# Turning a normalized tile on TensorE: GpSimd scales it before plain transposes, or TensorE multiplies by diagonals of 1/sigma

## Chip, cores and metric

The kernel runs on one core of a Trainium2 chip. The metric is the time of one execution on the device, in microseconds (us); a kernel's time is the median of several runs. TensorE is called PE here (PEld is its loading of weights), VectorE DVE, ScalarE ACT, GpSimd POOL and SyncE SP, as in the profile. L321 is line 321 of the kernel.

## What is computed

Two layers run one after the other on an input of 8 images of 128 x 128 positions with 128 channels, all in float32. The change lies in layer 0, an attention with a linear cost followed by a normalization over the channels:

```python
qkv = jnp.einsum('bhwc,cf->bhwf', x, w_qkv)
q, k, v = jnp.split(qkv, 3, axis=-1)          # 4 heads of 32
q = jax.nn.softmax(q, axis=-2) * inv_scale    # over the 32 of a head
k = jax.nn.softmax(k, axis=-1)                # over the positions of an image
context = jnp.einsum('bhdn,bhen->bhde', k, v)
attn = jnp.einsum('bhde,bhdn->bhen', context, q)
out = jnp.einsum('bhwf,fc->bhwc', attn, w_out) + b_out
mu = jnp.mean(out, axis=-1, keepdims=True)
var = jnp.mean(jnp.square(out - mu), axis=-1, keepdims=True)
out = (out - mu) * jax.lax.rsqrt(var + LN_EPS) * gamma + beta
return out + x
```

Layer 1 is a scan over the image in four orders (a selective state-space layer). It takes three quarters of the time, and the change doesn't touch it.

## The kernel before, in words

`layer0` keeps two images in SBUF, channels on the partitions (`xs`), and works on groups of 4 columns of 128 positions, that is on 128 x 512 tiles; an image has 32 groups. The function `image(b)` writes out by hand the order in which the stages of three images are interleaved: it attends to image `b`, it gathers the context (the product of keys and values) of image `b + 1`, and it computes the gate of image `b - 1`, which layer 1 needs. In step `t` it calls the stages for groups `t`, `t - 1`, `t - 2` and so on, so each group passes through several steps. `in_order` ties every instruction to the one before it on its engine, so each engine's queue holds exactly this order.

In one step PE gets these products, in this order: `pq` (L268, queries of group `t`), `pg` (L288, the exponentials of the queries times the output weights), `pk` (L180, keys of the next image), `pv` (L225, its values), `po` (L294, through the context), `pc` (L240, adds to the next image's context) and `pt` (L321, the turn). Each product of float32 appears as two records in the trace. All outputs of PE but `pc` and `pmx` rotate through 6 banks of PSUM.

The keys' softmax needs a maximum. Every four groups (`BK = 4`) the stages `fold` and `spread` take it: DVE reduces a tile (L196, L197), PE turns it (L206, `pmt`, a transpose), DVE reduces the result, joins it to the last maximum (L208, L210, L212), and writes a diagonal (L214, `dg`); PE spreads it over the partitions (L219, `pmx`). This is called a fold below.

A group's way through the attention is: `query` (PE L268; on DVE the maximum L270 and the subtraction L272), `exponent` (ACT L275), `normalize` (DVE L280, L281; POOL L282, which multiplies the tile by the reciprocals), `through_wo` (PE L288, ACT copy `gt` L290), `through_context` (PE L294; DVE adds the bias, L296, and writes the tile `o`; ACT squares it into `sq`, L298), `variance` (DVE L302), `scale` (POOL L308, L310, L313), `turn` (PE L321) and `finish` (ACT L325 applies gamma and beta, POOL L327 adds the input, and SP stores two groups at a time to DRAM, L330). The mean is taken out of the weights beforehand, so `o` has none.

After the normalization the tile must be turned, from positions on the partitions back to channels. Before the change, `scale` writes into a tile `d` four diagonal matrices that hold 1/sigma, one for each column of the group, and `turn` multiplies: the tile `o` of a column, as the stationary operand, times its diagonal gives the tile turned and scaled at once.

```python
i3 = ident.rearrange("p (o c) -> p o c", o=1)
nc.gpsimd.tensor_tensor(
    d, i3.to_broadcast([P, GW, P]), rstd.to_broadcast([P, GW, P]), ALU.mult
)
```

Image 0's context comes alone, before any attention. Images 0 to 6 have attention and context side by side: their 32 steps are called an image's loop, the last steps, in which the attention of the last groups ends and the context is completed, its drain. Image 7 has no next image; in its steps the gates of images 6 and 7 are interleaved instead. The gates of the images before (L157, L159) stand after the first step of each image.

Of the kernel before, what the change touches and what calls it, by code (L numbers as in the profile page):

```python
# [8 lines left out]
F32 = mybir.dt.float32  # L9
BF16 = mybir.dt.bfloat16  # L10
AF = mybir.ActivationFunctionType
ALU = mybir.AluOpType
# [4 lines left out]
P = 128  # L17
# [7 lines left out]
GW = 4  # L25
# [52 lines left out]
def layer0(ctx: ExitStack, tc, xT, w_qkv, w_out, b_out, gamma, beta, win, x1, zs):  # L78
# [12 lines left out]
    nc = tc.nc  # L91
    const = ctx.enter_context(tc.tile_pool(name="l0c", bufs=1))
    wp = ctx.enter_context(tc.tile_pool(name="l0w", bufs=2))
# [4 lines left out]
    ident = const.tile([P, P], F32, name="ident")  # L98
# [40 lines left out]
    def group(b, g):  # L139
        return xs[b % 2][:, g * GW : (g + 1) * GW, :]  # L140
# [120 lines left out]
    def attend(b):  # L261

        cn = ctxs[b % 2]
        qs, gs, os, vs, ys = {}, {}, {}, {}, {}

        def query(g):
            pq = ps.tile([P, GW * NH, HD], F32, name="pq", tag="ps")
            nc.tensor.matmul(pq, wq[:, 0:P], group(b, g), start=True, stop=True)  # L268
            qm = sm.tile([P, GW * NH, 1], F32, name="qm")
            nc.vector.tensor_reduce(qm, pq, AX.X, ALU.max)  # L270
            qs[g] = q = wp.tile([P, GW * NH, HD], F32, name="q", bufs=3)
            nc.vector.tensor_tensor(q, pq, qm.to_broadcast([P, GW * NH, HD]), ALU.subtract)  # L272

        def exponent(g):
            nc.scalar.activation(qs[g], qs[g], AF.Exp)  # L275

        def normalize(g):
            q = qs[g]
            t = sm.tile([P, GW * NH, 1], F32, name="qs")
            nc.vector.tensor_reduce(t, q, AX.X, ALU.add)  # L280
            nc.vector.reciprocal(t, t)  # L281
            nc.gpsimd.tensor_tensor(q, q, t.to_broadcast([P, GW * NH, HD]), ALU.mult)  # L282

        def through_wo(g):
            q = qs.pop(g).rearrange("p (w n) d -> p w (n d)", w=GW)
            pg = ps.tile([P, GW, P], F32, name="pg", tag="ps")
            for i in range(GW):
                nc.tensor.matmul(pg[:, i, :], q[:, i, :], wo, start=True, stop=True)  # L288
            gs[g] = gt = wp.tile([P, GW, P], F32, name="gt")
            nc.scalar.copy(gt, pg)  # L290

        def through_context(g):
            po = ps.tile([P, GW, P], F32, name="po", tag="ps")
            nc.tensor.matmul(po, cn, gs.pop(g), start=True, stop=True)  # L294
            os[g] = o = wp.tile([P, GW, P], F32, name="o", bufs=3)
            nc.vector.tensor_tensor(o, po, bb, ALU.add)  # L296
            vs[g] = sq = wp.tile([P, GW, P], F32, name="sq")
            nc.scalar.activation(sq, o, AF.Square)  # L298

        def variance(g):  # L300
            var = sm.tile([P, GW], F32, name="var")
            nc.vector.tensor_reduce(var, vs[g], AX.X, ALU.add)  # L302
            vs[g] = var

        def scale(g):

            var = vs[g]
            nc.gpsimd.tensor_scalar(var, var, 1.0 / P, EPS0, ALU.mult, ALU.add)  # L308
            rstd = sm.tile([P, GW, 1], F32, name="rstd")
            nc.gpsimd.tensor_tensor(rstd[:, :, 0], var, half, ALU.pow)  # L310
            vs[g] = d = wp.tile([P, GW, P], F32, name="d")
            i3 = ident.rearrange("p (o c) -> p o c", o=1)
            nc.gpsimd.tensor_tensor(  # L313
                d, i3.to_broadcast([P, GW, P]), rstd.to_broadcast([P, GW, P]), ALU.mult
            )

        def turn(g):
            o, d = os.pop(g), vs.pop(g)
            ys[g] = pt = ps.tile([P, GW, P], F32, name="pt", tag="ps")
            for i in range(GW):  # L320
                nc.tensor.matmul(pt[:, i, :], o[:, i, :], d[:, i, :], start=True, stop=True)  # L321

        def finish(g):
            y = wp.tile([P, GW, P], F32, name="x1t")
            nc.scalar.activation(y, ys.pop(g), AF.Identity, bias=gb[:, 1:2], scale=gb[:, 0:1])  # L325
            xg = group(b, g)
            nc.gpsimd.tensor_tensor(xg, y, xg, ALU.add)  # L327
            if g % 2 == 1:
                t = xs[b % 2][:, (g - 1) * GW : (g + 1) * GW, :].rearrange("p w h -> p (w h)")
                nc.sync.dma_start(x1[ORDER[b]][:, (g - 1) * GN : (g + 1) * GN], t)  # L330

        return query, exponent, normalize, through_wo, through_context, variance, scale, turn, finish

    def image(b):
# [875 lines left out]
```

## Time and profile before

| | us |
|---|---|
| median of 3 runs | 9561.42 |
| lowest and highest run | 9554.78, 9563.56 |
| the profiled execution: its span | 9556.3 |
| layer 0 within it | 0 to 2352 |
| busy over the whole span: DVE | 8129.7 (85%) |
| ACT, POOL | 7202.0, 7192.2 (75% each) |
| PE | 6281.6 (66%) |

The times of the runs are those of the whole execution on the device; the span goes from the first to the last instruction of one profiled execution. In the profile, a row of the timeline gives the start, the duration, the engine, the line, the operation, the output and its inputs, the number of instructions merged into the row, and in brackets the idle time of the engine before it and what ended that. A row of the waits gives who waited for whom, the total in us, how many times, and the longest. A row of the table of stretches gives the stretch, its length, the busy time of PE, PEld, DVE, ACT and POOL with the number of instructions, the mean clock that PE was granted (1.00 is full speed), the busy share of the DMA engines and the GB/s. Products on PE are pipelined: one ends later than the next begins, so the duration of one is longer than the time for which it holds the engine.

### The profile page before, as it was taken

The numbers are of one execution on the slowest core, as the hardware profiler recorded it, in microseconds if no ns is written. First come the engines' busy times: TensorE is split into PE (matmuls) and PEld (weight loads), VectorE is DVE, ScalarE is ACT, GpSimd is POOL, SyncE is SP. The second block draws the span as 40 slices with busy tenths as digits, with TensorE's granted clock in tenths as the row PEclk, the third lists the DMA queues.
The fourth block names the chain that finished last, engine by engine and source line by source line (L and its number), as shares of the span: only waits on it lengthen the run. The fifth ranks groups of instructions, "written<-read, shape, count | busy, mean of one in ns | idle before, by whom it ended". The sixth has DMA issues, their size and how long they took to land. (4 is left out here: it accounts for less than half of the span.)

```text
span 9556.3 us, 89734 instructions
## 1 busy us (share of the span) xinstructions
PE 6281.6 (66%) x24190; PEld 3101.4 (32%) x24352; DVE 8129.7 (85%) x8188; ACT 7202.0 (75%) x8288; POOL 7192.2 (75%) x4361
## 2 busy tenths in 40 slices
PE   8999999898977788777823544636345363543636
PEld 5556655554322233222300311404123040220403
DVE  6667765564988889888979999999999999999996
ACT  5556555567877788777878788888888888888884
POOL 3445544455665578776859999999999999999997
PEclk9999999999988899888955665757557585665857
DMA  2332233313476678987765957759487685867858
GB/s 91 135 133 81 95 133 132 133 71 140 172 266 232 229 262 247 266 263 269 243 204 165 257 174 207 240 174 269 154 228 219 186 260 165 244 190 198 245 165 212
DMA packets 1034807, 1851.21 MB, mean 194 GB/s; under 512 B 274852, under 2 KB 500772, under 8 KB 1026112
## 3 DMA queue, kind: packets, MB, share of 16 engines
q1 hardware_dynamic: 999488, 1711.23, 54.2%
q0 software_dynamic: 34816, 134.23, 7.3%
q8 instruction: 199, 3.26, 0.1%
q14 instruction: 304, 2.49, 0.1%
HBM read 1153.03 MB, written 692.12 MB: 193 GB/s over the span
## 5 line engine op out<-in xcount | busy, mean ns | idle before, releaser
L893 POOL TENSOR_TENSOR ubt<-ubt,sp 128x1024 f32<-128x1024 f32 x1024 | 2457.9, 2458 | 161.0 <-ACT sp L886 74.3
L882 PE MATMUL px<-rows,dtw 128*128 128x512 bf16 x1893 | 909.5, 573 | 2271.7 <-DVE y L943 1063.5
L515 POOL TENSOR_TENSOR tap<-tap 128x1024 f32<-128x1024 f32 x512 | 1206.1, 2367 | 640.1 <-ACT tap L513 517.9
L523 DVE SCALAR_TENSOR_TENSOR acc<-xb,cw,acc 128x1024 f32<-128x1024 f32 x1024 | 1320.6, 1290 | 52.7 <-ACT tap L513 0.9
L886 ACT ACTIVATE sp<-px 128x1024 f32<-128x1024 f32 x1024 | 1046.0, 1024 | 420.7 <-PE px L882 265.6
L951 POOL TENSOR_TENSOR y<-y,ubt 128x512 f32<-128x512 f32 x768 | 1160.0, 1557 | 142.9 <-DVE ubt L924 141.9
L505 PE MATMUL acc<-xi,wt 128*128 128x512 f32 x2048 | 952.2, 608 | 383.9 <-ACT ures L530 383.6
L903 DVE TENSOR_TENSOR_SCAN ubt<-px,ubt 128x1024 f32<-128x1024 f32 x512 | 1177.0, 2332 | 25.9 <-POOL ubt L893 19.2
L901 DVE TENSOR_TENSOR_SCAN ubt<-px,ubt 128x1024 f32<-128x1024 f32 x512 | 1178.3, 2332 | 14.1 <-POOL ubt L893 6.3
L882 PEld LDWEIGHTS <-dtw 128*128 128x128 bf16 x2048 | 163.9, 109 | 3066.2 <-issue 865.9
L890 ACT ACTIVATE px<-sp,sa 128x1024 f32<-128x1024 f32 x1024 | 1110.2, 1109 | 6.1
L513 ACT ACTIVATE tap<-xb,cw 128x1024 f32<-128x1024 f32 x768 | 834.0, 1139 | 68.1 <-POOL tap L515 67.8
L282 POOL TENSOR_TENSOR q<-q,qs 128x512 f32<-128x512 f32 x256 | 271.2, 1060 | 691.5 <-DVE qs L281 691.5
L886 ACT ACT_TABLE_LOAD x512 | 656.9, 1283 | 164.5 <-PE px L882 129.2
L505 PEld LDWEIGHTS acc<-xi,wt 128*128 128x128 f32 x2048 | 383.6, 192 | 928.3 <-ACT ures L530 486.1
L890 ACT ACT_TABLE_LOAD x512 | 656.9, 1283 | 9.2
L1016 PEld LDWEIGHTS px<-wg,z 128*128 128x128 f32 x4096 | 553.8, 218 | 118.6 <-issue 113.5
L909 PE MATMUL pc<-rows,csel 128*128 128x512 bf16 x1017 | 512.7, 585 | 88.9 <-DVE rstd L1004 79.9
L1016 PE MATMUL px<-wg,z 128*128 128x128 f32 x4096 | 554.1, 301 | 0.0
L478 PE MATMUL pxb<-xi,wi 128*128 128x512 f32 x1024 | 495.9, 606 | 4.3 <-ACT xb L487 4.3
L943 DVE TENSOR_TENSOR y<-y,px 128x1024 f32<-128x1024 f32 x384 | 468.7, 1221 | 14.7 <-DVE px L931 0.5
L298 ACT ACTIVATE sq<-o 128x512 f32<-128x512 f32 x256 | 161.2, 630 | 418.2 <-DVE o L296 416.9
(155 smaller groups left out, 15187.7 us busy)
## 6 DMA issues: line engine op xcount, KB each, us to landing
ubt<-ubs SPq DMA_DIRECT2D x512, 1024.0 KB
zs<-z SPq DMA_DIRECT2D x512, 256.0 KB
ubs<-ures SPq DMA_DIRECT2D x256, 512.0 KB
ubs<-turned SPq DMA_DIRECT2D x256, 512.0 KB
z<-zs SPq DMA_DIRECT2D x256, 512.0 KB
y<-gs POOLq DMA_DIRECT2D x128, 1024.0 KB, 10.5
rows<-xps SPq DMA_DIRECT2D x1536, 60.0 KB
xi<-x SPq DMA_DIRECT2D x120, 576.0 KB
```

The costliest lines, as they stand in the source:

```text
L505: nc.tensor.matmul(acc[:, s, :], wt[:, j, c, :], x, start=(j == 0), stop=(j == len(ON_PE) - 1))
L513: nc.scalar.activation(t, at(n, c, *d), AF.Copy, scale=cw[:, c, tap(*d) : tap(*d) + 1])
L515: nc.gpsimd.tensor_tensor(sums[n, c], sums[n, c], t, ALU.add)
L523: nc.vector.scalar_tensor_tensor(acc, at(n, c, *d), cw[:, c, tap(*d) : tap(*d) + 1], acc, ALU.mult, ALU.add)
L882: nc.tensor.matmul(p[:, hf * 512 : hf * 512 + 512], sl.dw[:, c * P : c * P + P], src, start=True, stop=True)
L886: nc.scalar.activation(t, da[n, c], AF.Softplus)
L890: nc.scalar.activation(da[n, c], sp[n, c], AF.Exp, scale=sa[:, sl.s, c : c + 1])
L893: nc.gpsimd.tensor_tensor(ubt[n][:, c, :], ubt[n][:, c, :], sp.pop((n, c)), ALU.mult)
L901: nc.vector.tensor_tensor_scan(e[:, ::-1], x[:, ::-1], e[:, ::-1], start, ALU.mult, ALU.add)
L903: nc.vector.tensor_tensor_scan(e, x, e, start, ALU.mult, ALU.add)
L951: nc.gpsimd.tensor_tensor(v[:, c], v[:, c], h[:, c], ALU.add)
L1016: nc.tensor.matmul(po[:, w, :], z[:, c, w * H : w * H + H], wg[:, c, :], start=(c == 0), stop=(c == NC2 - 1))
```

## The change

In `scale`, GpSimd no longer multiplies the identity by 1/sigma into a tile of its own, `d`. It multiplies the tile `o` itself by 1/sigma, in place. In `turn`, TensorE turns each column of `o` by a transpose against the identity, in place of the product with the diagonal. The tile `d` and its two buffers are gone. The other stages and the order of the stages stay as they are.

```diff
         def scale(g):
 
-            var = vs[g]
+            var = vs.pop(g)
             nc.gpsimd.tensor_scalar(var, var, 1.0 / P, EPS0, ALU.mult, ALU.add)
             rstd = sm.tile([P, GW, 1], F32, name="rstd")
             nc.gpsimd.tensor_tensor(rstd[:, :, 0], var, half, ALU.pow)
-            vs[g] = d = wp.tile([P, GW, P], F32, name="d")
-            i3 = ident.rearrange("p (o c) -> p o c", o=1)
-            nc.gpsimd.tensor_tensor(
-                d, i3.to_broadcast([P, GW, P]), rstd.to_broadcast([P, GW, P]), ALU.mult
-            )
+            o = os[g]
+            nc.gpsimd.tensor_tensor(o, o, rstd.to_broadcast([P, GW, P]), ALU.mult)
 
         def turn(g):
-            o, d = os.pop(g), vs.pop(g)
+            o = os.pop(g)
             ys[g] = pt = ps.tile([P, GW, P], F32, name="pt", tag="ps")
             for i in range(GW):
-                nc.tensor.matmul(pt[:, i, :], o[:, i, :], d[:, i, :], start=True, stop=True)
+                nc.tensor.transpose(pt[:, i, :], o[:, i, :], ident)
```

## The prediction

> **What bounds the kernel now.** The change touches layer 0 alone, the first 2352 of 9556.3 us, so I read that stretch first: by the table of stretches, then, inside one image's loop, who waits for whom, then the timeline of one fold.
>
> ```profile
> 0.00:2352.00 2352.00, 2126.88 (x9408) 1300.08 (x9408) 1489.93 (x2596) 1436.33 (x2438) 1154.72 (x1286) 0.98 0.30 115
> ...
> 1010.00:1176.00 166.00, 158.78 (x829) 108.31 (x827) 139.00 (x240) 103.60 (x186) 114.86 (x128) 1.00 0.11 42
> ```
>
> The columns are length, then busy PE, PEld, DVE, ACT, POOL, granted clock, DMA. PE is busy for 90% of layer 0 and 96% of a loop; DVE follows with 84%. That reads like a kernel bound by PE. The waits in the same 166 us say otherwise (first DVE's, then PE's):
>
> ```profile
> DVE var L302 <- ACT sq L298: 17.7, 25, 1.1
> ```
> ```profile
> PE pmx L219 <- DVE dg L214: 7.0, 6, 1.3
> PE pg L288 <- POOL q L282: 0.2, 1, 0.2
> ```
>
> DVE never waits for PE. It waits only for the squares on ACT, which come from its own sums: a loop of DVE and ACT. PE waits for DVE, once in four groups. The timeline of one such fold:
>
> ```profile
> 1105.76 0.58 ACT L290 COPY gt<-pg 128x512 f32<-128x512 f32 x1
> ...
> 1107.37 1.04 POOL L313 TENSOR_TENSOR d<-ident,rstd 128x512 f32<-128x512 f32 x1
> ...
> 1107.85 1.05 PE L240 MATMUL pc<-vt,k 128*128 128x129 f32 x8
> ...
> 1108.74 1.06 PE L321 MATMUL pt<-d,o 128*128 128x128 f32 x8
> ...
> 1109.60 1.04 POOL L282 TENSOR_TENSOR q<-q,qs 128x512 f32<-128x512 f32 x1
> 1109.69 0.97 DVE L212 TENSOR_TENSOR a<-m 128x1 f32<-128x1 f32 x1
> 1110.58 0.28 DVE L214 TENSOR_SCALAR dg<-ident,m 128x128 f32<-128x128 f32 x1
> ...
> 1110.91 0.49 PE L219 MATMUL pmx<-dg,ones 128*128 128x128 f32 x2 [1.11 <-DVE dg L214]
> ...
> 1111.23 1.02 PE L268 MATMUL pq<-x,wq 128*128 128x512 f32 x2
> ...
> 1112.81 0.68 DVE L270 TENSOR_REDUCE qm<-pq 128x16 f32<-128x512 f32 x1
> ```
>
> The sum on DVE (L296) starts at 1084.62 and, four groups on, at 1110.78: a cycle of 26.16 us. PE enters it after the wait for dg, and the group's pq is done 0.56 us before DVE's maximum (L270) asks for it; in the next three groups 0.33, 0.11 and 1.40 us before. PE is just quick enough, so DVE sets the pace. In the last image (2100 to 2320) the group takes 8.7 us; PE waits there for ACT (L290) and POOL (L282), and pq is ready 2.85 us early.
>
> [...] Half-clock stretches begin whole multiples of 3.41 us apart. With windows cut on that grid, each of the 16 full-clock windows of layer 0 with at most 1.44 us of busy PE is followed by half clock, and none with 1.62 or more. The same place in the drains of two images:
>
> ```profile
> 607.95:611.36 3.41, 1.61 (x10) 1.05 (x8) 2.01 (x7) 2.50 (x5) 1.64 (x3) 1.00 0.29 113
> 611.36:614.78 3.42, 2.72 (x18) 2.24 (x19) 0.69 (x1) 1.35 (x3) 2.49 (x3) 1.00 0.00 0
> 894.67:898.08 3.41, 1.35 (x10) 0.92 (x8) 2.00 (x6) 2.35 (x5) 1.90 (x3) 1.00 0.20 80
> 898.08:901.50 3.42, 2.98 (x11) 2.63 (x12) 0.44 (x1) 0.78 (x1) 1.62 (x2) 0.50 0.00 0
> ```
>
> The grid fell so that the second lost its clock; from that image's last pq to the next image's first took 27.0 us, in the others 25.6. [...]
>
> **The change, part by part.**
>
> *Products become transposes.* L321 has 8 records per group, last start (1.06 - 0.275) / 7 = 0.112 us apart each, so it holds PE for 0.89 us. Five transposes of the same shape (L616) ran at half clock (0.50 in the table of stretches):
>
> ```profile
> 2639.45 1.30 PE L616 MATMUL ptx<-ident,xw 128*128 128x128 f32 x5 [9.15 <-DMA xw<-xds]
> ```
>
> One takes 0.42, so they start (1.30 - 0.42) / 4 = 0.22 apart, 0.11 at full clock. Four hold PE for 0.44: 0.45 us less per group, 115 us over 256 groups. Inside the loops nothing of it is gained, since DVE does not wait for PE. It turns into PE idle time ahead of pmx.
>
> *The drains.* In each of images 0 to 6 (at 1186.02 in this one), PE waits 2.50 us for POOL, turns, then does pmx, for which DVE waits 2.63 us. Here the 0.45 lies on the path: 7 x 0.45 = -3 us.
>
> *POOL.* The nearest row to o times rstd (a full tile and a broadcast one) is L282, 1061 ns against L313's 1039: +0.02. The other end is two full operands, L327, 1273: +0.23. DVE's L212 (0.97 us[...]) ends with POOL's L282[...]. So POOL's lateness passes to DVE once per fold: 56 x 0.02 = +1 us, at most +13.
>
> *Waits.* Built, both programs issue the same operations in the same order, and no DMA moves. DVE's sum (L296) now waits for PE and POOL, hence takes a separate semaphore instruction ahead of it; the POOL event is three groups old. It runs while the max before it (0.69 us) or dg (0.28) still works: nothing. Uncovered, it would cost as much as for L272, which starts 0.07 us later for it: 256 x 0.07 = 18 us. Behind the sum stand sq, var and the rest of the loop. POOL's multiplication waits for ACT's square, which var has already waited for.
>
> *The new idle time.* This decides. Nothing on DVE, ACT or POOL moves earlier, so in the fold above dg still ends at 1110.86 and pmx still starts at 1110.91. Rid of its backlog, PE is ahead of that: po starts when gt ends (1106.34) and takes 0.96 with its load, pc 0.89, to 1108.25; d ends at 1108.41; the transposes run from 1108.46 to about 1109.0. Then 1.9 us of nothing. Up to 0.16 of modelled tail after each group counts as busy in the profile's figures. If transposes do not count, 1108.41 to 1110.91 is 2.5 us of idle, and a window of 3.41 falls to 0.9 us busy, far below 1.44. If they do, it falls to 1.60, between the two bounds.
>
> How often: a window under 1.53 needs 1.88 of the 2.5 us idle, so (3.41 + 2.5 - 2 x 1.88) / 3.41 = 0.63 of the grid's positions hit. A cycle is 26.16 / 3.41 = 7.66 windows; one delayed by a hit (27.0) is 7.92, so the next fold stands nearly where this one stood and hits come in runs. I take 3 in 4 of the 49 inner folds (7 images, 7 each): 37.
>
> What one costs: with half clock from pmx on, pmx holds PE for 0.45 instead of 0.22 and pq takes 1.91 to its end (as at 1267.88, at half clock) instead of 1.02: 1.12 later, less the 0.56 of margin, so qm starts 0.55 late. The products of pg, most of them slow too, end 1.6 late; gt on ACT and exp(q), which stands behind it there, start after them, exp by 1.17 late. DVE is the bound, so this stays lost: 1.2 us. If the spell starts 1.5 us after pmx, 0.2. Mean over the positions 0.85. 37 x 0.85 = +31. In the drains I add two more spells of 1.4: +3.
>
> Sum: -3 + 1 + 31 + 3 = +32. On the profiled execution, 9556.3 + 32 = 9588; this span stands 5 us under the median of the runs, so 9561.4 + 32 = 9593.
>
> **Rivals.**
> *A, half clock at the folds (the forecast)*: 9593. From few hits to 56 x 1.1: +20 to +57, so 9581 to 9618. For: 16 of 16 windows, the 27.0 drain. Against: that transposes count as idle is not shown here.
> *B, the saving is hidden and the clock holds* (not slower): transposes count, the worst window stays at 1.60, above the true threshold. Then -3 + 1: 9559. It decides whether any window with a fold in it drops below about 1.5 us.
> *C, PE is the bound after all*: the margin of 0.11 us ahead of qm would be a modelled end, and DVE would wait for PE. Full size 115 us, 9446. Against: four groups of DVE without a wait, and ACT's exp starts 0.03 us after q in every group.
> *D, the change does not do what it says* (four transposes hold PE as long as eight products): no new idle and no spell, 9561 + 1. L616 nearly excludes it; it goes with B.
>
> **How the numbers follow.** A 0.68, B with D 0.27, C 0.05. Of A I count nearly all as slower by over 0.2% (19 us, about what a measurement here can tell from no change): slower 0.67, same 0.28, faster 0.05. The range joins A to B with the 4 us by which runs differ: 9555 to 9618. It leaves out C and a tenth of A.
>
> **What would show it.** Right: in the loops the granted clock falls below 1.00, folds where it does have PE at 0.5 after pmx, DVE shows waits for PE at qm or for ACT at qs, four groups take about 27 us instead of 26.16, L318 has 4 records per group, and layer 1 is as long as before. Wrong: clock 1.00 throughout the loops (B), cycles below 26 us (C), POOL's product over 1.1 us, or a difference that arises after 2352 us.

## The result and the profile after

The changed kernel takes 9580.83 us (median; before, run beside it on the same chip, 9557.87). The ratio is 1.0025, interval 1.0018 to 1.0032: slower by 17 to 31 us, where 32 were forecast. The profiled execution spans 9572.6 us, 16.3 more than that of before.

First, where in the span it went. I cut both traces at DVE's maximum over the queries (L270): at that of each image's second group, the first behind the gates, and at that of its last group.

| part of the span | before | after | difference |
|---|---|---|---|
| the loops of images 0 to 6 | 1383.0 | 1404.0 | +21.0 |
| between them (drain, gates, start of the next) | 570.6 | 568.6 | -2.0 |
| image 7 | 258.0 | 257.7 | -0.2 |
| layer 1, from its first instruction on POOL | 7203.9 | 7202.4 | -1.5 |

So the loss is made inside the loops. The table of stretches after, columns as before (length, busy PE, PEld, DVE, ACT, POOL, clock, DMA share, GB/s):

```profile
0.00:2370.50 2370.50, 2076.99 (x8384) 1192.09 (x8384) 1495.83 (x2598) 1433.11 (x2438) 1156.26 (x1288) 0.96 0.30 114
1010.00:1176.00 166.00, 152.67 (x701) 95.09 (x699) 136.84 (x235) 99.56 (x178) 112.50 (x126) 0.97 0.11 42
```

In the same 166 us PE lost 6.1 us of busy time, as the change meant, but its clock is 0.97, where it was 1.00. The waits of this stretch, DVE's and then PE's:

```profile
DVE var L302 <- ACT sq L298: 17.3, 25, 1.0
DVE qs L280 <- ACT q L275: 3.0, 4, 0.8
DVE o L296 <- PE po L294: 0.3, 1, 0.3
```
```profile
PE pmx L219 <- DVE dg L214: 9.6, 6, 1.8
PE pg L288 <- POOL q L282: 1.6, 2, 1.0
```

PE's wait for dg has grown, up to 1.8 us. DVE has a wait that it did not have in this stretch: the group's row sum (`qs`) waits for the exponential on ACT, four times. The first of the four, at 1016.00, belongs to the start of the loop (before has it too, at 1004.20). The other three stand behind the three folds of this stretch that have half clock. Here is the window that holds the idle time of a fold, and the window after it, for two folds. They are cut on this trace's grid: its 38 half-clock stretches (called spells from here on) up to 2360 us all begin whole multiples of 3.413 us apart, within 0.001 us:

```profile
1067.43:1070.84 3.41, 1.56 (x11) 1.13 (x11) 3.28 (x7) 1.56 (x3) 2.67 (x3) 1.00 0.00 0
1070.84:1074.25 3.41, 3.41 (x12) 2.38 (x11) 2.41 (x5) 1.39 (x3) 1.64 (x3) 0.50 0.02 5
...
1149.35:1152.76 3.41, 1.62 (x8) 0.95 (x8) 2.71 (x7) 1.39 (x3) 2.00 (x2) 1.00 0.00 0
1152.76:1156.17 3.41, 3.41 (x15) 2.03 (x14) 3.04 (x5) 2.61 (x7) 2.31 (x4) 1.00 0.00 0
```

Behind 1.56 us of busy PE the next window has a clock of 0.50; behind 1.62 it has 1.00. It is the same in all seven loops: 20 of the windows ahead of a spell hold 1.55 to 1.59 us, one holds 1.62, and every window that kept the clock after it holds 1.62 or more. So after has 21 spells in the loops (4, 4, 3, 3, 1, 3 and 3 by image), before has none; they are counted from an image's second sum (L296) to its last, since the start of every image has one more in both kernels. Within an image they mostly come 27.3 us apart, eight windows of the grid. The timeline of the fold at the first pair of windows, with rows left out between those shown:

```profile
1066.83 1.04 POOL L312 TENSOR_TENSOR o<-o,rstd 128x512 f32<-128x512 f32 x1
1067.93 0.66 PE L318 MATMUL pt<-ident,o 128*128 128x128 f32 x4
1069.06 1.04 POOL L282 TENSOR_TENSOR q<-q,qs 128x512 f32<-128x512 f32 x1
1069.15 0.97 DVE L212 TENSOR_TENSOR a<-m 128x1 f32<-128x1 f32 x1
1070.04 0.27 DVE L214 TENSOR_SCALAR dg<-ident,m 128x128 f32<-128x128 f32 x1
1070.37 0.49 PE L219 MATMUL pmx<-dg,ones 128*128 128x128 f32 x2 [1.79 <-DVE dg L214]
1070.69 1.77 PE L268 MATMUL pq<-x,wq 128*128 128x512 f32 x2
1072.25 1.91 PE L288 MATMUL pg<-wo,q 128*128 128x128 f32 x8
1072.50 0.69 DVE L270 TENSOR_REDUCE qm<-pq 128x16 f32<-128x512 f32 x1
1073.29 0.69 DVE L272 TENSOR_TENSOR q<-pq,qm 128x512 f32<-128x512 f32 x1
1074.26 0.59 ACT L290 COPY gt<-pg 128x512 f32<-128x512 f32 x1 [1.86 <-PE pg L288]
1074.74 0.63 ACT L275 ACTIVATE q<-q 128x512 f32<-128x512 f32 x1
1075.41 0.69 DVE L280 TENSOR_REDUCE qs<-q 128x16 f32<-128x512 f32 x1 [0.83 <-ACT q L275]
```

The same three rows of before, behind the fold that the prediction shows:

```profile
1113.60 0.69 DVE L272 TENSOR_TENSOR q<-pq,qm 128x512 f32<-128x512 f32 x1
1114.33 0.63 ACT L275 ACTIVATE q<-q 128x512 f32<-128x512 f32 x1 [0.50 <-DVE q L272]
1114.99 0.69 DVE L280 TENSOR_REDUCE qs<-q 128x16 f32<-128x512 f32 x1
```

Read it from dg to the row sum on DVE. Before, dg ended at 1110.86, qm began at 1112.81, and qs (L280) at 1114.99: 4.13 us. Here dg ends at 1070.31, qm begins at 1072.50, and qs at 1075.41: 5.10 us, 0.97 more. 0.24 of it comes by way of pq, which is slow; the rest by way of pg: `gt` waits 1.86 us for it on ACT, and the exponential, which stands behind `gt` in ACT's queue, starts 0.76 after its subtraction has ended, where it started at once before. DVE sets the pace of the loop, so this stays lost. Two cycles of four groups, cut from the sum (L296) behind one fold to the sum behind the next; the first has the spell above, the second has none:

```profile
1070.24:1097.33 27.09, 25.23 (x115) 16.34 (x115) 22.24 (x40) 16.08 (x29) 18.00 (x20) 0.94 0.10 40
1151.48:1177.65 26.17, 24.23 (x115) 14.99 (x115) 22.01 (x40) 16.27 (x29) 17.95 (x20) 1.00 0.10 41
```

The spell costs 0.92 us. Of the 42 such cycles in the loops, 19 have a spell and take 27.08 us (median); 23 have none and take 26.16, as before. 21 spells of 0.92 to 0.97 us are 19 to 20 us: nearly all of the 21.0 us lost in the loops.

### The profile page after: what moved, and what is told of

It is laid out like the page before. It is cut to its first block, busy times and chain, and to the rows that moved or that the text cites. A ratio compares the mean times of both kernels' runs of the same rounds, so it can differ in the third digit from the quotient of the medians.

```text
span 9572.6 us, 88058 instructions
## 1 busy us (share of the span) xinstructions
PE 6273.4 (66%) x23328; PEld 2995.1 (31%) x23328; DVE 8133.9 (85%) x8188; ACT 7199.8 (75%) x8288; POOL 7195.4 (75%) x4361
## 5 line engine op out<-in xcount | busy, mean ns | idle before, releaser
L879 PE MATMUL px<-rows,dtw 128*128 128x512 bf16 x2048 | 954.4, 565 | 2241.3 <-DVE y L940 1044.7
L520 DVE SCALAR_TENSOR_TENSOR acc<-xb,cw,acc 128x1024 f32<-128x1024 f32 x1024 | 1320.7, 1290 | 52.7 <-ACT tap L510 0.9
L282 POOL TENSOR_TENSOR q<-q,qs 128x512 f32<-128x512 f32 x256 | 271.5, 1061 | 701.0 <-DVE qs L281 696.6
```

The costliest lines, as they stand in the source:

```text
L520: nc.vector.scalar_tensor_tensor(acc, at(n, c, *d), cw[:, c, tap(*d) : tap(*d) + 1], acc, ALU.mult, ALU.add)
L879: nc.tensor.matmul(p[:, hf * 512 : hf * 512 + 512], sl.dw[:, c * P : c * P + P], src, start=True, stop=True)
```

## The experiments

My theory: the idle time that the transposes leave on PE halves its clock at some folds, and DVE, the bound, gets its inputs late. Rivals: POOL's multiplication or the new waits cost the time; or PE does wait less, and the gain is lost elsewhere. A second question is whether transposes count as busy for the clock. This table sums up all runs. A cycle is four groups in a loop, cut as above; the column gives the median of 42, and for `after` both kinds, without and with a spell (in e3 and e4 the median falls among those with one). Spells are those in the loops. Each ratio is to the kernel before as run beside that kernel (9555.17 to 9557.92 us).

| kernel | cycle, us | spells | time, us | ratio to before |
|---|---|---|---|---|
| before | 26.16 | 0 | 9557.87 | |
| after | 26.16, 27.08 | 21 | 9580.83 | 1.0025 (1.0018 to 1.0032) |
| e1_twice | 26.17 | 0 | 9558.32 | 0.9997 (0.9989 to 1.0006) |
| e2_pool_part | 26.16 | 0 | 9558.1 | 1.0000 (0.9992 to 1.0008) |
| e3_pe_part | 27.07 | 26 | 9566.88 | 1.0010 (1.0002 to 1.0018) |
| e4_turn_last | 27.58 | 33 | 9606.74 | 1.0049 (1.0037 to 1.0062) |
| e5_spread_late | 26.16 | 0 | 9553.41 | 0.9998 (0.9990 to 1.0006) |
| e6_relief_products | 24.74 | 0 | 9491.54 | 0.9928 (0.9915 to 0.9940) |
| e7_relief_transposes | 24.59 | 0 | 9483.73 | 0.9920 (0.9907 to 0.9934) |
| e8_relief_late | 24.59 | 0 | 9480.41 | 0.9919 (0.9905 to 0.9932) |
| e9_no_max_products | 24.79 | 0 | 9460.70 | 0.9906 (0.9893 to 0.9920) |
| e10_no_max_transposes | 23.35 | 1 | 9397.00 | 0.9835 (0.9822 to 0.9849) |

**Filling the idle time (e1_twice).** The kernel after, each transpose done twice:

```diff
-            for i in range(GW):
+            for i in [*range(GW), *range(GW)]:
```

> The changed kernel with the four transposes of each group issued twice, into the same bank: PE is held for 0.88 us per group again, as by the products before, and everything else is as after the change. If the loss comes from spells of half clock after idle time at the folds, and transposes count as busy for the clock, the emptiest window of a fold holds about 2.0 us of busy PE instead of 1.6, no spell is left in the loops, and the time is that of before: ratio 1.000 (0.999 to 1.001). If transposes do not count, the window stays as empty as after the change and the spells stay: 1.0025 or more. If the loss comes from the product on POOL or from the added wait on DVE, it stays too: 1.0025, with the clock at 1.00 in the loops.

The time is that of before (0.9997), and all 21 spells are gone. The loop stretch, a window ahead of a fold with the next one, and then the first of these two windows for the transposes alone (PE, PEld, ACT):

```profile
1010.00:1176.00 166.00, 158.28 (x821) 106.83 (x820) 139.31 (x242) 104.00 (x186) 114.99 (x128) 1.00 0.11 42
...
1057.03:1060.44 3.41, 2.05 (x18) 1.73 (x17) 3.21 (x8) 1.67 (x4) 2.79 (x3) 1.00 0.00 0
1060.44:1063.85 3.41, 3.41 (x16) 2.01 (x15) 2.55 (x5) 2.32 (x5) 1.52 (x3) 1.00 0.00 0
```
```profile
1057.03:1060.44 3.41, 1.09 (x8) 0.86 (x8) 0.00 (x0) 1.00 0.00 0
```

More work on PE made the kernel faster (9558.32 us for 9580.83). That leaves nothing for POOL's product or the waits, which are the same as after. It also answers the second question. Without the transposes this window holds 2.05 - 1.09 = 0.96 us of busy PE, far below the 1.44 up to which every window of before was followed by half clock. The clock of the next window is 1.00: here the transposes counted. The loading of weights that belongs to each transpose was doubled with it; the two were not told apart.

**POOL's part alone (e2_pool_part).** POOL scales `o`, and PE turns it by products with the identity:

```diff
-                nc.tensor.transpose(pt[:, i, :], o[:, i, :], ident)
+                nc.tensor.matmul(pt[:, i, :], o[:, i, :], ident, start=True, stop=True)
```

> One part alone: POOL multiplies the tile o by 1/sigma in place, as after the change, and PE turns it by products with the identity (8 records per group, 0.89 us). The theory of the clock expects no spells in the loops and the time of before, ratio 1.000, plus at most 1 us for POOL. The rival, that POOL's product or the second semaphore that DVE's sum waits for costs the time, expects the whole loss here: 1.0025.

Ratio 1.0000, cycle 26.16. POOL's new product, and DVE's sum with one more semaphore to wait for, cost nothing that can be measured. The rival falls.

**PE's part alone (e3_pe_part).** The kernel before with transposes; the tile `d` is still made, but not used, so this kernel leaves out the division by sigma:

```diff
-                nc.tensor.matmul(pt[:, i, :], o[:, i, :], d[:, i, :], start=True, stop=True)
+                nc.tensor.transpose(pt[:, i, :], o[:, i, :], ident)
```

> The other part alone: PE turns by transposes, and POOL still writes the diagonals of 1/sigma into d, which nobody reads, so the layer leaves the division by sigma out. The theory of the clock expects all of the loss, 1.0025 (1.001 to 1.004), with about 20 spells of 3.4 us in the loops. The rival of POOL and the wait expects 1.000 or a little less.

```profile
1010.00:1176.00 166.00, 152.63 (x713) 96.74 (x711) 137.47 (x237) 101.80 (x181) 112.36 (x126) 0.97 0.10 39
```

26 spells; the loops are 22.0 us longer than before (after: 21.0). The total is only 9 us up, at the low end of what was expected: the turn no longer needs a result of POOL, and the time between the loops, where it waited for one in each drain, falls from 570.6 to 557.5. The loss in the loops belongs to the transposes.

**Idle time in one piece (e4_turn_last).** The kernel after with the same work in another order: pmx ahead of the turn, so that the turn no longer splits PE's idle time.

```diff
+            at(spread, a - 1)
             at(turn, t - 2)
...
-            at(spread, a - 1)
```

> The changed kernel with only the order changed: at a fold, pmx comes before the turn on PE instead of after it. No work is added. PE's idle time ahead of pmx is then in one piece, from the end of pc to the end of dg, 2.5 us, and a window with all of it in holds about 0.9 us of busy PE, well under 1.5. pq still comes in time for DVE, 0.1 us ahead. The theory of the clock expects more spells than after the change, 30 to 45 in the loops against 21, at about 1 us each: ratio 1.0035 to 1.0055. If the loss has another cause, the order of these two doesn't matter: 1.0025.

```profile
1102.92:1106.33 3.41, 0.91 (x9) 0.72 (x8) 3.30 (x7) 1.48 (x3) 2.59 (x3) 1.00 0.01 2
1106.33:1109.74 3.41, 3.41 (x13) 2.38 (x12) 1.64 (x3) 1.40 (x3) 1.72 (x3) 0.50 0.00 0
```
```profile
1105.78 0.49 PE L219 MATMUL pmx<-dg,ones 128*128 128x128 f32 x2 [2.50 <-DVE dg L214]
1106.10 0.83 PE L318 MATMUL pt<-ident,o 128*128 128x128 f32 x4
1106.73 1.92 PE L268 MATMUL pq<-x,wq 128*128 128x512 f32 x2
1108.68 0.69 DVE L270 TENSOR_REDUCE qm<-pq 128x16 f32<-128x512 f32 x1 [0.92 <-PE pq L268]
```

The window ahead of the fold falls to 0.91 us, the one idle time is 2.50 us, and there are 33 spells instead of 21. The loops are 50.7 us longer than before: 1.5 us per spell, more than the 1 us expected, because the turn now stands, slow too, between pmx and pq, and DVE waits 0.92 us for pq. More idle time in one place, more spells: the dose goes with the effect.

**Idle time spread out (e5_spread_late).** The kernel after with pmx behind the next group's pq, so that PE has pq to do while dg is made:

```diff
             at(query, t)
+            at(spread, a - 2)
...
-            at(spread, a - 1)
```

> The changed kernel with pmx (stage spread) moved behind the next group's query product on PE, with the small exp on ACT that belongs to it. PE then has pq to do while DVE finishes dg, so the idle time ahead of pmx falls from 1.9 to about 1.0 us in one piece. The theory of the clock, with the threshold that the runs so far show (about 1.2 to 1.3 us of the 3.41 spent on products, transposes included), expects no spell in the inner folds, four groups in 26.16 us, and a ratio of 0.9992 to 1.0003. If PE's idle time were harmless and something else cost the 21 us in the loops, they would stay: 1.0025.

```profile
1107.09:1110.50 3.41, 2.48 (x15) 1.46 (x13) 3.20 (x8) 2.08 (x4) 3.20 (x3) 1.00 0.00 0
1110.50:1113.91 3.41, 3.35 (x15) 2.17 (x16) 2.55 (x6) 1.86 (x4) 1.19 (x2) 1.00 0.01 2
```
```profile
PE pmx L219 <- DVE dg L214: 5.6, 6, 0.9
PE pg L288 <- POOL q L282: 5.5, 8, 0.8
```

The window ahead of the fold holds 2.48 us, no wait of PE is over 0.9 us, and no spell is left. PE is still idle for 11.9 of these 166 us (before: 7.2), only in smaller pieces. The time is that of before, not less (0.9998): the time that the transposes free is worth nothing in the loop, because DVE sets the pace.

**Relieving DVE (e6, e7, e8).** To see when the freed time is worth something, I took work off DVE at the fold: one reduction in place of two maxima of two inputs (L196, L197), the joined maximum with one tensor input (L210), and the subtraction (L212) moved into ACT's exponential. e6 is this on the kernel before, e7 on the kernel after, e8 is e7 with the move of e5.

```diff
-                nc.vector.tensor_tensor(run[:, 0:2], run[:, 0:2], run[:, 2:4], ALU.max)
-                nc.vector.tensor_tensor(run[:, 0], run[:, 0], run[:, 1], ALU.max)
+                runs[j] = top = wp.tile([P, P], F32, name="top")
+                nc.vector.tensor_reduce(top, run.rearrange("p w c -> p c w"), AX.X, ALU.max)
...
-                nc.vector.tensor_tensor(m, m, ms[j - 1], ALU.max)
-                scales[j] = a = sm.tile([P, 1], F32, name="a")
-                nc.vector.tensor_tensor(a, ms.pop(j - 1), m, ALU.subtract)
+                old = ms.pop(j - 1)
+                nc.vector.tensor_scalar(m, m, old, None, ALU.max)
+                scales[j] = old, m
...
-                    nc.scalar.activation(scales[j], scales[j], AF.Exp)
+                    old, m = scales[j]
+                    scales[j] = a = sm.tile([P, 1], F32, name="a")
+                    nc.scalar.activation(a, m, AF.Exp, bias=old, scale=-1.0)
```

> The kernel before the change (products with diagonals), with less work for DVE at a fold: the maximum over a tile in one reduction instead of two steps, the joined maximum with a scalar operand, and the difference of the maxima left to ACT's exp as its bias. This should take about 2.0 us off DVE per fold (0.77 + 0.34 + 0.89 by the timeline of before). If DVE sets the pace and PE is just quick enough, the cycle of four groups falls from 26.16 only to PE's own 25.1 us (4 x 6.11 for the seven products plus 0.11 + 0.22 for the fold, and waits): about 50 us less, ratio 0.995, with PE now the bound and its clock at 1.00. If PE were the bound all along, nothing is gained: 1.000.

> The changed kernel (transposes) with the same relief for DVE. PE needs 25.1 - 4 x 0.45 = 23.3 us per cycle and DVE 24.2, so the cycle falls to 24.2 to 24.5 and the idle time ahead of pmx, which ends 1.2 us earlier, to under 1 us: few spells or none. Ratio 0.989 to 0.992, that is 30 to 50 us below the same relief with products: there the transposes would gain what they could not gain before. If spells of half clock remain in the loops, up to 20 us of it are lost; if the transposes can gain nothing wherever DVE stands, the ratio is that of the relief with products or above.

> As the relief with transposes, with pmx behind the next group's query product besides. If spells cost anything with the relief, this takes them away, 0.989 to 0.991; if there are none, it is the same as with pmx in its old place, within 0.0005.

e6 gains 66 us (about 50 expected), the cycle falls to 24.74 us (25.1 expected). That shows DVE as the bound of the kernel before. Its loop stretch, and PE's only wait in it:

```profile
982.00:1130.00 148.00, 147.79 (x775) 101.04 (x774) 122.48 (x215) 98.30 (x175) 107.36 (x121) 1.00 0.11 43
```
```profile
PE pg L290 <- POOL q L284: 0.2, 1, 0.2
```

PE is busy for 147.79 of 148.00 us and waits 0.2: now PE is the bound. With transposes on top (e7) I expected 30 to 50 us more and got 8: a miss. The relief took 1.57 us per fold off the cycle, where I had counted 2.0, so DVE, at 24.59, stands right behind PE, at 24.74. No spell came: PE's waits for dg in e7 reach only 0.7 us. e8, with pmx moved, is equal to e7 as expected.

**PE as the bound (e9, e10).** One step more off DVE: the queries' maximum and its subtraction are left out, and ACT takes the exponential straight from pq. e9 is this on e6 (products), e10 on e7 (transposes).

```diff
-            qm = sm.tile([P, GW * NH, 1], F32, name="qm")
-            nc.vector.tensor_reduce(qm, pq, AX.X, ALU.max)
-            qs[g] = q = wp.tile([P, GW * NH, HD], F32, name="q", bufs=3)
-            nc.vector.tensor_tensor(q, pq, qm.to_broadcast([P, GW * NH, HD]), ALU.subtract)
+            qs[g] = pq
...
-            nc.scalar.activation(qs[g], qs[g], AF.Exp)
+            pq = qs[g]
+            qs[g] = q = wp.tile([P, GW * NH, HD], F32, name="q", bufs=3)
+            nc.scalar.activation(q, pq, AF.Exp)
```

> The kernel before (products with diagonals) with the relief at the folds, and besides with the queries' maximum left out: ACT takes the exponential straight from PSUM, so DVE does neither the maximum nor the subtraction (0.60 us each per group). The softmax is the same but for rounding. DVE then needs about 4.7 us per group and PE 6.11, so PE is the bound: about 24.8 us per four groups, no more than 0.1 us per cycle below the relief alone, clock 1.00. Ratio 0.992 to 0.994 (the relief with products alone: 0.9928).

> The same relief with transposes. Where PE is the bound, each group is 0.45 us shorter: 24.8 falls to about 23.1 us per four groups. Over 7 loops of about 28 groups that is 7 x 28 x 0.45 = 88 us, less what POOL (4.7 us per group) or the chain of one group takes back: ratio 0.983 to 0.986, with the clock at 1.00 in the loops, since PE has no idle time to lose it by. The rival, that transposes gain nothing here even when PE is the bound (dearer in a row than at L616, or half clock again), expects the ratio of the products, 0.992 to 0.994.

```profile
966.00:1113.00 147.00, 147.00 (x776) 101.17 (x776) 95.29 (x166) 94.12 (x173) 106.16 (x119) 1.00 0.11 44
```
```profile
938.00:1077.00 139.00, 138.13 (x680) 89.69 (x679) 91.39 (x168) 92.64 (x174) 107.25 (x120) 1.00 0.11 45
```

The first row is e9: PE busy in all of 147.00 us, DVE in 65%. Its cycle is that of e6, as expected; its ratio, 0.9906, is a little better than the 0.992 to 0.994 expected, so something outside the inner cycles became shorter too, which I did not follow up. The second is e10. Between them lies the change of this document, and here it gains 64 us: 1.44 us per cycle, 0.36 per group. So the transposes are worth having, and the change as such is no mistake; it is worth nothing while DVE is the bound. e10 is the fastest of all, 158 us under the kernel before, though it drops the guard against overflow that the maximum gives.

## Why the prediction was right, and where it was not

The sign, the place and the path were right; the number of spells was not. Too many spells (37 for 21) at too small a cost (0.85 us for 0.92 to 0.97) partly cancelled.

- **The bound.** Read from the waits, not from the busy share: DVE. e5 (spells gone, nothing gained) and e6 (66 us from DVE's work) show it. Rival C (PE the bound, 9446) falls.
- **"One takes 0.42, so they start 0.11 apart. Four hold PE for 0.44."** Right: L318 has 4 records of 0.273 us, which start 0.109 apart (medians of the stretch) and last 0.60 to 0.66 us in all, and the stretch shows 6.1 us less of busy PE. With PE as the bound (e10 against e9) 0.36 us per group came out, where 0.45 was counted.
- **The drains, -3, and two spells there, +3.** Together 0 was forecast. From the last group's maximum to the first of the next image DVE took 26.08 us before and takes 25.52 after where no spell falls, 0.56 less where 0.45 was counted. In the drains spells begin at 330.2, 910.4 and 1200.5, where before had one, at 898.1: two more, as counted, at 1.66 us each instead of 1.4. The seven together came out 0.4 us shorter; the other 1.6 us between the loops lie behind the next image's first maximum, where no change was forecast.
- **POOL, +1.** The new product takes 1039 ns, as the old one did, so 0. e2 bounds it together with the waits at less than 0.1% of the time, some 8 us.
- **The separate semaphore ahead of DVE's sum, 0.** After has it at 238 of the 256 sums (21 ns each), before at none; in both the sum begins 0.08 us before the instruction ahead of it ends (median). So 0, within the same bound (e2); the 18 us of an uncovered one lie outside it.
- **The step that failed: "If transposes do not count, ... a window of 3.41 falls to 0.9 us busy, far below 1.44."** I took this as the likely branch; that was an estimate, and no trace of before showed it. The measurement decides against it for these float32 transposes. e1 shows it directly. The traces of before and after say it again: in layer 0, from 25 us after its start to its last turn, they hold 1290 windows at full clock on the grid, of which 55 are followed by half clock. I counted PE's time at the distance at which records follow each other (0.432 us for a 128x512 record, 0.109 for a transpose), which leaves out the modelled tails. With transposes counted, one bound of 1.28 us sorts them with 3 exceptions; without, the best bound (0.85) leaves 12.
- **Hence the other branch: "If they do, it falls to 1.60, between the two bounds."** That is what happened: 1.55 to 1.59 in the windows ahead of the spells, between the 1.44 and the 1.62 of before. I had put the clock's holding on this branch (rival B), and it did not hold. That the sign came out right on the other branch is in part luck: the windows of folds that kept the clock held 1.62 us, only 0.05 more. Since even the worst-placed window falls only just under 1.62, nearly the whole idle time of 1.79 us must lie in one window. By this estimate (3.41 - 1.79) / 3.41 = 0.47 of the grid's positions are hit, 23 of 49 folds; 21 were, where 37 were forecast.
- **"Mean over the positions 0.85."** Measured 0.92 to 0.97. In the fold shown, 0.24 came by pq (0.55 forecast for a spell that begins with pmx; this one began at 1070.84, 0.47 later) and the rest by pg and the exponential behind `gt`, the way that the forecast gave for most of it.
- **"56 x 1.1: +20 to +57."** A slip in the sum: 56 x 1.1 is 62, so with the drains and POOL the range of A ends at +60. Nothing here hangs on it.

The loops' term was thus +21.0, of which 21 spells make 19 to 20, where 37 x 0.85 = +31 was forecast. With -2.0 between the loops, -0.2 in image 7, -1.5 in layer 1 and -1.1 ahead of the first cut and behind the last it makes the 16.3 us between the two profiled executions; the medians lie 23 us apart. What stays open: why a window with 1.62 us in image 6 (2019.75) lost the clock when others with 1.62 kept it. Such figures differ by less than the modelled ends of products can be trusted.

## What to carry to other kernels

Before making an engine quicker, read who waits for it: PE was busy for 96% of the loop and still not the bound, so freed PE time became idle time. Here idle PE time was not free. Where the change left PE a window of 3.41 us with 1.55 to 1.59 us of busy time, the work after it ran at half clock (20 of the 21 spells, which together cost 19 to 20 us); split that idle time by the order of the work (e5), or first relieve the engine that sets the pace and take the saving after that (e10).

## What was not expected of the hardware

- Float32 transposes kept the clock up here as products did: in e1 a window with 0.96 us of other work and 1.09 us of transposes was followed by a clock of 1.00, where in layer 0 of before every window with at most 1.44 us of busy PE was followed by 0.50. Whether the transposes by themselves did it or their weight loads stays open.
- The clock fell behind windows that were not idle: in after, 20 windows with 1.55 to 1.59 us of busy PE of 3.41 were followed by 0.50. In the fold shown, 1.79 us of the window were one idle stretch.
- The spells keep themselves going: a spell makes the cycle 27.1 us, close to eight windows (27.3), so the next fold meets the same place on the grid (in image 3 they begin at 1070.84, 1098.15 and 1125.45). Without one it is 26.16 us, 7.66 windows, and the fold moves along the grid.
- A subtraction of two 128x1 columns on DVE (L212) took 0.97 us in the 42 folds in which POOL's L282 (128x512) ran beside it, and ended 0.01 to 0.02 us after that; in the other 14 it took 0.16, in 7 of them with POOL at L310 (128x4) and in 7 with POOL idle. The counts are the same in before and after. Taking it and the two-input maxima off DVE was worth the 66 us of e6.
